# Splitting an RWKV stage into three pieces and emitting a block's channel mix behind the next block's time mix

## The chip, the cores and the metric

The kernel runs on one core of a Trainium2 chip. Its time is the device time of one execution in microseconds, the median of the runs shown. In this text PE is the matrix engine, DVE the vector engine, ACT the scalar engine, POOL the general engine (GpSimd), and SP the engine that only issues DMAs here.

## What is computed

An activation `x` of 64 sequences x 32 steps x 256 channels goes through six layers, each added to `x` (float32):

```python
x = x + L0_xattn(layernorm(x), ctx, ...)   # stage 0: cross attention over 257 context rows
x = x + L0_attn(layernorm(x), ...)         # stage 1: RWKV, the layer that the change is in
x = x + L0_ffn(layernorm(x), ...)          # stage 2: top-2 experts
x = x + L1_xattn(layernorm(x), ctx, ...)   # stage 3: quantized grouped attention
x = x + L1_attn(layernorm(x), ...)         # stage 4: Mamba
x = x + L1_ffn(layernorm(x), ...)          # stage 5: top-1 experts
```

RWKV has two halves. The time mix blends each step with the step before it, projects to k, v and r, runs a recurrence along the 32 steps in each channel, and multiplies by sigmoid(r); an output projection Wo is added to the normalized input. The channel mix normalizes that sum, blends with the step before again, and adds sigmoid(Wcr xr) * (Wcv relu(Wck xk)^2), where Wck goes from 256 to 1024 channels and Wcv back.

## The kernel before

The 2048 tokens are cut into four blocks of 512 tokens (16 sequences), as `x[b]`, 128 partitions x 4 x 256, which stay on the chip for the whole program. Each stage is a function that returns a `block(b)`; `layers` (from L1188) calls them in a written order. The blocks don't depend on each other, the stages of one block do.

What sets the order on the engines: each engine works its own queue in order. At build, a planner fills the queues from the instructions as they are emitted. Among those whose inputs and buffers are ready by its own cost figures, the one emitted first goes first. So the written order is a rank, not the order itself: in the trace matmuls of stage 0 and stage 1 stand in PE's queue in turns. A tile of a pool with `bufs=n` and a tag shares n buffers with the other tiles of that tag, and an instruction that takes a buffer waits for its last user. A stage's pools are opened on the left or the right side of the memory, and what is opened later on a side waits until the space is released.

Stage 0 (L136 to L321): a block loads four pieces of context (cn, cT; two buffers each), computes scores, a softmax and a weighted sum, and adds to x at L283. It also writes a quantized context and its step sizes to DRAM, which stage 3 reads. Its pools stand on the right side, so the weights of stages 2 and 3 can be loaded when its last block is done.

Stage 1 (L340 to L531), for a block: moments of x (DVE) and a reciprocal root (POOL and DVE); `norm_to` (L418) normalizes into rows `hn` (L429, DVE), transposes on PE (L123) and evacuates to `hT` (L422, ACT), a buffer that holds channels x 16 sequences x 33 steps with a zero ahead; `shift_mix` (L391) makes the difference `d` (L398) and the blends (L408) on DVE; `recur` (L432), once for each half of the channels, projects on PE (L415), evacuates on ACT (L435, L437, L439), and runs the recurrence on DVE with three scans (L443, L457, L458), a reciprocal (L464) and elementwise steps up to `rw` (L468), with products on POOL (L449, L461, L467); the output projection Wo (L490, PE), added on DVE (L491); a second norm and blend; the gate `sg` (L503 PE, L504 ACT). Then the channel mix: eight times a matmul pair L511 on PE, a relu L513 on ACT, a square L514 on POOL, and four matmuls L523 on PE into two banks; at the end the gate's product L528 on DVE and the sum L529 on POOL. Its pools stand on the left side, where stage 4 follows: stage 4's weights can be loaded when stage 1's last block has released the space.

Stage 2 (L537) adds its experts to x at L616. Stage 3 (L653) ends a block at L748. Stage 4 (L918) has a long recurrence that begins at L1036, stage 5 (L1081) writes the output.

The order in `layers`: stage 0 of block 0, then stage 0 of block b followed by stage 1 of block b - 1 while b is 1 or 2, stage 0 of block 3, the step sizes, stage 2 and stage 3 of block 0, stage 1 of blocks 2 and 3, and then stage 4's pools, stage 2 of block 1 and the rest.

Of the kernel before, what the change touches and what calls it, by code (L numbers as in the profile page):

```python
# [8 lines left out]
F32 = mybir.dt.float32  # L9
# [6 lines left out]
P = 128  # L16
NB, T, S, D = 64, 32, 257, 256
NTOK = NB * T
NT = NTOK // P
NBLK = 4  # L20
# [319 lines left out]
def _stage1(k, pool):  # L340
# [2 lines left out]


    nc, i = k.nc, k.i
    w, u, wk, sm1 = pool("w1", 1), pool("u1", 9), pool("wk1", 1), pool("small1", 2)
    pa, pb = pool("psa1", 2, space=bass.MemoryType.PSUM), pool("psb1", 2, space=bass.MemoryType.PSUM)
    wT = {n: _load_w(k, w, f"L0_attn_W{n}T", 2, D) for n in ("k", "v", "r", "o", "cr")}
    wck = _load_w(k, w, "L0_attn_WckT", 2, 4 * D)
# [11 lines left out]
    def padded(name, fill, shape=(16, T + 1)):  # L361
        t = w.tile([P, *shape], F32, name=name, tag=name)
        nc.gpsimd.memset(t, fill)
        return t

    wt, kp, e1b, e2b, e2bv = [], [], [], [], []
    for c in range(2):
        wt.append(padded(f"wt{c}", BIG))
        nc.vector.tensor_copy(wt[c][:, :, 1:], wdec[:, c : c + 1].unsqueeze(2).to_broadcast([P, 16, T]))
        kp.append(padded(f"kp{c}", BIG))  # L370
        e1b.append(padded(f"e1b{c}", 0.0))
        e2b.append(padded(f"e2b{c}", 0.0))
        e2bv.append(padded(f"e2bv{c}", 0.0))
    hT = padded("hT", 0.0, (2, 16, T + 1))

    def seq(t):
        return t.rearrange("p b t -> p (b t)")
# [8 lines left out]
        return pa.tile([P, BT], F32, name=name, tag="a")  # L386

    def rows(name):
        return wk.tile([P, 4, D], F32, name=name, tag="rows", bufs=3)

    def shift_mix(names):  # L391


        def mix(name):
            return wk.tile([P, 2, 16, T], F32, name=name, tag="mix", bufs=3)

        d = mix("d")
        nc.vector.tensor_tensor(  # L398
            d.rearrange("p c b t -> p (c b) t"),
            hT[:, :, :, 1:].rearrange("p c b t -> p (c b) t"),  # L400
            hT[:, :, :, 0:T].rearrange("p c b t -> p (c b) t"),
            ALU.subtract,
        )
        outs = []
        for n in names:
            o = d if n == names[-1] else mix("mix")
            for c in range(2):
                nc.vector.scalar_tensor_tensor(o[:, c], d[:, c], _chan(k, n, c), hT[:, c, :, 0:T], ALU.mult, ALU.add)  # L408
            outs.append(o.rearrange("p c b t -> p c (b t)"))
        return outs  # L410
# [4 lines left out]
            nc.tensor.matmul(p, wT[wname][:, c, o * P : (o + 1) * P], xT[:, c, :], start=c == 0, stop=c == 1)  # L415
        return p.rearrange("p (b t) -> p b t", t=T)

    def norm_to(xs, mean, scale, g, b):  # L418


        def evac(c, p):
            nc.scalar.activation(  # L422
                hT[:, c, :, 1:], p.rearrange("p (b t) -> p b t", t=T), AF.Identity,
                bias=_chan(k, b, c), scale=_chan(k, g, c),
            )

        hn = rows("hn")
        for j in range(4):
            nc.vector.tensor_scalar(hn[:, j, :], xs[:, j, :], mean[:, j, :], scale[:, j : j + 1], ALU.subtract, ALU.mult)  # L429
        _to_channels(k, [hn[:, j, :] for j in range(4)], evac, lambda shape, name: ps(name))  # L430
# [36 lines left out]
        nc.gpsimd.tensor_tensor(sr, sr, den, ALU.mult)  # L467
        nc.vector.tensor_tensor(rw[:, c].rearrange("p (b t) -> p b t", t=T), num, sr, ALU.mult)  # L468

    def block(b):  # L470
        x = k.x[b]
        xs = [x[:, j, :] for j in range(4)]


        mv = _moments(k, xs, "1", sm1)
        r8 = sm1.tile([P, 8], F32, name="r8", tag="r8")
        _rsqrt(k, r8, [(mv[:, :, 1], 1.0, LN_EPS), (mv[:, :, 1], 1.0 + LN_EPS, LN_EPS * LN_EPS)], "1", sm1)
        norm_to(x, mv[:, :, 0:1], r8[:, 4:8], "L0_attn_ln1_g", "L0_attn_ln1_b")
        xk, xv, xr = shift_mix(["L0_attn_tm_k", "L0_attn_tm_v", "L0_attn_tm_r"])
        rw = wk.tile([P, 2, BT], F32, name="rw", tag="rw", bufs=1)  # L480
        for c in range(2):
            recur(c, xk, xv, xr, rw)
        xn = rows("xn")
        for j in range(4):
            nc.gpsimd.tensor_scalar(xn[:, j, :], xs[j], mv[:, j, 0:1], r8[:, j : j + 1], ALU.subtract, ALU.mult)
        for j in range(0, 4, 2):
            p = pb.tile([P, 2, D], F32, name="wo", tag="b")
            for f in range(2):
                for c in range(2):
                    nc.tensor.matmul(p[:, f, :], rw[:, c, (j + f) * P : (j + f + 1) * P], wT["o"][:, c, :], start=c == 0, stop=c == 1)  # L490
            nc.vector.tensor_tensor(xn[:, j : j + 2, :], p, xn[:, j : j + 2, :], ALU.add)  # L491

        nc.gpsimd.tensor_tensor(x, x, xn, ALU.add)

        mv2, rstd2 = _stats(k, [xn[:, j, :] for j in range(4)], "1b", sm1)
        norm_to(xn, mv2[:, :, 0:1], rstd2, "L0_attn_ln2_g", "L0_attn_ln2_b")
        xk, xr = shift_mix(["L0_attn_cm_k", "L0_attn_cm_r"])
        sg = rows("sg")
        for j in range(0, 4, 2):
            p = pa.tile([P, 2, D], F32, name="cr", tag="a")  # L500
            for f in range(2):
                for c in range(2):
                    nc.tensor.matmul(p[:, f, :], xr[:, c, (j + f) * P : (j + f + 1) * P], wT["cr"][:, c, :], start=c == 0, stop=c == 1)  # L503
            nc.scalar.activation(sg[:, j : j + 2, :], p, AF.Sigmoid)  # L504

        cvs = [pb.tile([P, 2, D], F32, name="cv", tag="b") for _ in range(2)]

        def up(h):
            p = ps("ck")
            for c in range(2):  # L510
                nc.tensor.matmul(p, wck[:, c, h * P : (h + 1) * P], xk[:, c, :], start=c == 0, stop=c == 1)  # L511
            kk = wk.tile([P, BT], F32, name="kk", tag="kk", bufs=3)
            nc.scalar.activation(kk, p, AF.Relu)  # L513
            nc.gpsimd.tensor_tensor(kk, kk, kk, ALU.mult)  # L514
            return kk

        ahead = [up(0), up(1)]
        for h in range(8):
            if h + 2 < 8:
                ahead.append(up(h + 2))  # L520
            kk = ahead.pop(0)
            for j in range(4):
                nc.tensor.matmul(  # L523
                    cvs[j // 2][:, j % 2, :], kk[:, j * P : (j + 1) * P], wcv[:, h, :],
                    start=h == 0 and j % 2 == 0, stop=h == 7, skip_group_check=True,
                )
        for j in range(0, 4, 2):
            nc.vector.tensor_tensor(sg[:, j : j + 2, :], cvs[j // 2], sg[:, j : j + 2, :], ALU.mult)  # L528
        nc.gpsimd.tensor_tensor(x, x, sg, ALU.add)  # L529

    return block  # L531

# [653 lines left out]
def layers(k, out):  # L1188

    def opened(es, side):
        def pool(name, bufs, **kw):
            return es.enter_context(k.tc.tile_pool(name=name, bufs=bufs, side=side, reuse_waits="tile", **kw))

        return pool

    psum = dict(space=bass.MemoryType.PSUM)
    left0, left, right, right2 = ExitStack(), ExitStack(), ExitStack(), ExitStack()  # L1200
    with left0:
        s1 = _stage1(k, opened(left0, "left"))
        with ExitStack() as es:
            s0, steps = _stage0(k, opened(es, "right"))
            s0(0)
            for b in range(1, NBLK):
                s0(b)
                if b < NBLK - 1:
                    s1(b - 1)
            steps()  # L1210
        pool = opened(right, "right")
        k.small, k.ps, w3 = pool("small1", 2), pool("ps", 2, **psum), pool("w3", 1)
        k.wk3 = pool("wk3", 2)
        with ExitStack() as es:
            s3 = _stage3(k, w3, opened(es, "right")("tmp3", 1))
        s2 = _stage2(k, opened(right2, "right"))
        s2(0)
        s3(0)
        s1(NBLK - 2)
        s1(NBLK - 1)  # L1220
    with right, left:
        pool = opened(left, "left")
        k.psh, k.psp, k.psu = pool("psh", 2, **psum), pool("psp", 1, **psum), pool("psu", 1, **psum)
        w4 = pool("w4", 1)
        ahead, gates, recur = _stage4(k, w4, pool("wk4", 2))
        with right2:
            s2(1)
            v = {0: ahead(0)}
            gates(v[0])
            s3(1)  # L1230
            s2(2)
            v[1] = ahead(1)
            recur(0, v[0])
            s3(2)
            s2(3)
        k.psacc, w5 = pool("psacc", 2, **psum), pool("w5", 1)
        s5 = _stage5(k, w5, out)
        k.wk5 = pool("wk5", 2)
        for b in range(1, NBLK):
            gates(v[b])  # L1240
            if b + 1 < NBLK:
                v[b + 1] = ahead(b + 1)
            recur(b, v[b])
            if b + 2 < NBLK:
                s3(b + 2)
            s5(b - 1)
        s5(NBLK - 1)
# [81 lines left out]
```

## Time and profile before

| what | us |
|---|---|
| median of 3 runs | 2092.72 |
| lowest and highest run | 2090.38, 2098.58 |
| the profiled execution's own time | 2096.84 |
| its span, first to last instruction | 2095.1 |
| busy in the span: PE, DVE, POOL, ACT | 1644.2, 1391.0, 1013.9, 952.6 |

The profile is of one execution of the program. Its views used here: busy time of each engine in a stretch of the span (the columns are the stretch, its length, then for each engine busy us and number of instructions, the granted share of PE's clock, the DMA share and GB/s); waits (who waited for whom, total us, times, the longest); groups of instructions by source line (out<-in, shapes, count, then busy us and mean ns, then idle time of the engine ahead of them and who ended it); one line's instructions (min/median/max ns, and the start of the first and last in us); and the chain of work that ended last. PEld is PE's weight load, which overlaps with matmuls. Ends of matmuls are modelled. L490 is line 490 of the kernel.

### The profile page before, as it was taken

What the parts mean: (1) busy time and instruction counts of PE and PEld (TensorE: products, weight loads), DVE (VectorE), ACT (ScalarE), POOL (GpSimd) and SP (SyncE); (2) the same over time, 40 slices, a digit from 0 to 9 for tenths busy, and PEclk for the clock granted to TensorE, in tenths of its full rate; (3) what the DMA queues carried; (4) which work ended last, traced back from release to release, by engine and by line L of the source; (5) the groups of instructions that cost most, each with busy time, mean ns of one, the idle gap of its engine ahead of it and who ended that gap; (6) DMA issues with size and microseconds to landing.
All of it is one profiled execution on the core that took longest, in us unless ns stands there. A gap on an engine that the chain in (4) does not pass through costs nothing. (4 is left out here: it accounts for less than half of the span.)

```text
span 2095.1 us, 20245 instructions
## 1 busy us (share of the span) xinstructions
PE 1644.2 (78%) x6455; PEld 834.1 (40%) x6455; DVE 1391.0 (66%) x2444; ACT 952.6 (45%) x2009; POOL 1013.9 (48%) x1037
## 2 busy tenths in 40 slices
PE   4778966669979788656487798887888987787798
PEld 2334534335545434433234344433444433233343
DVE  5587584775584559889767988655888755876100
ACT  3445342304434174444146566356557445664232
POOL 4445445312121325667625777513767634998000
PEclk8677977889989898558687899888799887999799
DMA  7654232210001011121011232112232112332021
GB/s 239 219 182 144 91 120 80 79 34 21 21 21 43 17 42 51 30 61 61 0 50 53 80 91 90 31 41 65 71 88 73 49 31 66 89 111 77 30 81 40
DMA packets 87540, 149.93 MB, mean 72 GB/s; under 512 B 7672, under 2 KB 51978, under 8 KB 85386
## 3 DMA queue, kind: packets, MB, share of 16 engines
q1 hardware_dynamic: 84868, 147.69, 23.0%
q10 hardware_dynamic: 2566, 0.96, 0.2%
q8 instruction: 51, 0.84, 0.2%
q14 instruction: 55, 0.45, 0.1%
HBM read 137.71 MB, written 10.91 MB: 71 GB/s over the span
## 5 line engine op out<-in xcount | busy, mean ns | idle before, releaser
L1048 POOL TENSOR_TENSOR g<-dtx,bc 128x1024 f32<-128x1024 f32 x128 | 300.4, 2353 | 194.8 <-DVE h L1053 89.4
L1053 DVE TENSOR_TENSOR_SCAN h<-h,g 128x512 f32<-128x512 f32 x256 | 307.3, 1218 | 49.9 <-ACT h L1052 35.1
L1160 PE MATMUL up<-xT,w 128*128 128x512 f32 x512 | 288.1, 678 | 42.5 <-ACT hid L1162 37.3
L1055 POOL TENSOR_TENSOR xc<-xc,hc 128x1024 f32<-128x1024 f32 x128 | 301.0, 2356 | 26.5 <-DVE hc L1054 14.8
L1168 PE MATMUL acc<-hid,w 128*128 128x512 f32 x512 | 250.9, 610 | 15.8 <-ACT hid L1164 15.7
L1052 ACT ACTIVATE h<-dt,A 128x512 f32<-128x512 f32 x256 | 174.0, 692 | 184.5 <-DVE hc L1054 183.3
L1054 DVE TENSOR_TENSOR hc<-h,bc 128x512 f32<-128x512 f32 x256 | 169.7, 679 | 2.9 <-POOL xc L1055 0.5
L1160 PEld LDWEIGHTS up<-xT,w 128*128 128x128 f32 x512 | 97.3, 209 | 165.3 <-issue 79.2
L839 ACT ACTIVATE p<-sc,nm 128x256 f32<-128x256 f32 x256 | 117.6, 471 | 94.5 <-DVE nm L835 83.2
L1162 ACT ACTIVATE hid<-up,chan 128x512 f32<-128x512 f32 x128 | 87.2, 681 | 159.5 <-PE up L1160 159.4
L614 PE MATMUL weps<-we,xT 128*128 128x512 f32 x256 | 139.3, 665 | 17.2 <-DVE x L616 13.9
L1168 PEld LDWEIGHTS acc<-hid,w 128*128 128x128 f32 x512 | 94.1, 194 | 128.2 <-issue 96.3
L828 PE MATMUL sc<-kT,qm 32*128 32x256 f32 x512 | 131.6, 448 | 14.9 <-DVE od L867 11.5
L852 PE MATMUL pt_ps<-ident,p 128*128 128x128 f32 x512 | 97.0, 328 | 53.7 <-ACT p L839 26.6
L833 DVE TENSOR_REDUCE nm<-sc 128x2 f32<-128x512 f32 x128 | 86.3, 686 | 56.2 <-PE sc L828 55.1
L89 POOL TENSOR_TENSOR rs_t<-rs_r 128x4 f32<-128x4 f32 (+3 forms) x138 | 29.7, 218 | 183.1 <-DVE rs_r L87 157.0
L852 PEld LDWEIGHTS pt_ps<-ident,p 128*128 128x128 f32 x512 | 69.5, 165 | 107.1 <-ACT p L839 64.4
L828 PEld LDWEIGHTS sc<-kT,qm 32*128 32x128 f32 x512 | 81.5, 208 | 70.5 <-DVE od L867 20.7
L230 POOL TENSOR_TENSOR cT<-cT,scb 128x2056 f32<-128x2056 f32 x16 | 74.5, 4657 | 53.5 <-DMA scb<-scales 51.8
L1181 DVE SCALAR_TENSOR_TENSOR o<-rT,gt,x 128x256 f32<-128x256 f32 x16 | 7.7, 483 | 139.4 <-PE rT L1180 132.5
L854 ACT COPY pt<-pt_ps 128x512 f32<-128x512 f32 x128 | 74.0, 588 | 40.5 <-PE pt_ps L852 40.3
L514 POOL TENSOR_TENSOR kk<-kk 128x512 f32<-128x512 f32 x32 | 33.1, 1040 | 103.8 <-ACT kk L513 103.8
(389 smaller groups left out, 3218.7 us busy)
## 6 DMA issues: line engine op xcount, KB each, us to landing
bc<-rows SPq DMA_DIRECT2D x64, 512.0 KB
w<-in_L_ffn_w_dram SPq DMA_DIRECT2D x64, 512.0 KB
cT<-in_ctxT_dram SPq DMA_DIRECT2D x16, 1028.0 KB
cq<-cq SPq DMA_DIRECT2D x32, 514.0 KB
cn<-in_ctx_dram SPq DMA_DIRECT2D x64, 256.0 KB
scb<-scales SPq DMA_DIRECT2D x16, 514.0 KB
kb<-steps SPq DMA_DIRECT2D x16, 514.0 KB
x<-in_x_dram SPq DMA_DIRECT2D x4, 512.0 KB
```

Source lines behind the costliest of these rows:

```text
L614: nc.tensor.matmul(ps, xT[:, c, r], we[:, c, e : e + 2, :], start=c == 0, stop=c == 1)
L828: nc.tensor.matmul(sc[h][:, f, :], qm[r, e + f].rearrange("p l n g -> p (l n g)"), kTs[e][r, f, :], start=True, stop=True,)
L839: nc.scalar.activation(w_[:, f, h - h0, :], sc[h][:, f, :], AF.Exp, bias=nm[:, e + f, h : h + 1], accum_out=sm[:, e + f, h : h + 1],)
L852: nc.tensor.transpose(pt_ps[:, h, m, :], ws[e0, hp][:, f, h, m * P : (m + 1) * P], k.ident)
L1048: nc.gpsimd.tensor_tensor(g, dtx[:, c2 : c2 + 2], bc[:, 0:1, :].to_broadcast([P, 2, BT]), ALU.mult)
L1052: nc.scalar.activation(h, dt, AF.Exp, scale=A[:, c2 + c, n : n + 1])
L1053: nc.vector.tensor_tensor_scan(h, h, g[:, c, :], 0.0, ALU.mult, ALU.add)
L1054: nc.vector.tensor_tensor(hc[:, c, :], h, bc[:, 1, :], ALU.mult)
L1055: nc.gpsimd.tensor_tensor(y[:, c2 : c2 + 2], y[:, c2 : c2 + 2], hc, ALU.add)
L1160: nc.tensor.matmul(u, w1[e][:, c, q * P : (q + 1) * P], xT[:, c, :], start=c == 0, stop=c == 1)
L1162: nc.scalar.activation(hid[e][:, q, :], u, AF.Identity, bias=b1)
L1168: nc.tensor.matmul(acc[o], w2[e][:, q, o * P : (o + 1) * P], hid[e][:, q, :], start=n == H, stop=n == E * H + H - 1)
```

## The change

Stage 1's block function becomes three: `time_mix` (moments, norm, blend and recurrence), `between` (Wo, second norm, second blend, gate) and `channel_mix`. In `layers` the channel mix of block b - 1 is emitted behind the time mix of block b and ahead of the middle piece of block b. Stage 1 of a block is now emitted right behind stage 0 of the same block, ahead of stage 0 of the next one; stage 1 of block 2 up to its middle piece goes ahead of stage 0 of block 3; the time mix of block 3 and the channel mix of block 2 go between stages 2 and 3 of block 0; and stage 2 of block 1 goes ahead of the last channel mix and of stage 4's pools.

Buffers: `hT` gets a second copy, one for each norm. The rows (three buffers) and the blends (three buffers) share one tag with six. The recurrence's tiles have eight buffers, not nine. `e2bv` is one buffer for both halves of the channels, not two.

```diff
-    w, u, wk, sm1 = pool("w1", 1), pool("u1", 9), pool("wk1", 1), pool("small1", 2)
+    w, u, wk, sm1 = pool("w1", 1), pool("u1", 8), pool("wk1", 1), pool("small1", 2)
...
-        e2bv.append(padded(f"e2bv{c}", 0.0))
-    hT = padded("hT", 0.0, (2, 16, T + 1))
+        e2bv.append(e2bv[0] if c else padded("e2bv", 0.0))
+
+    hTs = [padded(f"hT{n}", 0.0, (2, 16, T + 1)) for n in range(2)]
...
     def rows(name):
-        return wk.tile([P, 4, D], F32, name=name, tag="rows", bufs=3)
-
-    def shift_mix(names):
+        return wk.tile([P, 4, D], F32, name=name, tag="rows", bufs=6)
+
+    def shift_mix(hT, names):
...
-            return wk.tile([P, 2, 16, T], F32, name=name, tag="mix", bufs=3)
+            return wk.tile([P, 2, 16, T], F32, name=name, tag="rows", bufs=6)
...
-    def block(b):
+    def time_mix(b):
...
-        norm_to(x, mv[:, :, 0:1], r8[:, 4:8], "L0_attn_ln1_g", "L0_attn_ln1_b")
-        xk, xv, xr = shift_mix(["L0_attn_tm_k", "L0_attn_tm_v", "L0_attn_tm_r"])
+        norm_to(hTs[0], x, mv[:, :, 0:1], r8[:, 4:8], "L0_attn_ln1_g", "L0_attn_ln1_b")
+        xk, xv, xr = shift_mix(hTs[0], ["L0_attn_tm_k", "L0_attn_tm_v", "L0_attn_tm_r"])
         rw = wk.tile([P, 2, BT], F32, name="rw", tag="rw", bufs=1)
         for c in range(2):
             recur(c, xk, xv, xr, rw)
+        return mv, r8, rw
+
+    def between(b, mv, r8, rw):
...
+        norm_to(hTs[1], xn, mv2[:, :, 0:1], rstd2, "L0_attn_ln2_g", "L0_attn_ln2_b")
+        xk, xr = shift_mix(hTs[1], ["L0_attn_cm_k", "L0_attn_cm_r"])
...
+        return xk, sg
+
+    def channel_mix(b, xk, sg):
+        x = k.x[b]
...
-        s1 = _stage1(k, opened(left0, "left"))
+        time_mix, between, channel_mix = _stage1(k, opened(left0, "left"))
         with ExitStack() as es:
             s0, steps = _stage0(k, opened(es, "right"))
-            s0(0)
-            for b in range(1, NBLK):
+
+            for b in range(NBLK - 1):
                 s0(b)
-                if b < NBLK - 1:
-                    s1(b - 1)
+                t = time_mix(b)
+                if b:
+                    channel_mix(b - 1, *c)
+                c = between(b, *t)
+            s0(NBLK - 1)
             steps()
...
         s2(0)
+        t = time_mix(NBLK - 1)
+        channel_mix(NBLK - 2, *c)
         s3(0)
-        s1(NBLK - 2)
-        s1(NBLK - 1)
+        c = between(NBLK - 1, *t)
+        s2(1)
+        channel_mix(NBLK - 1, *c)
...
         with right2:
-            s2(1)
             v = {0: ahead(0)}
```

## The prediction

> **What bounds the kernel now.** The page comes first. No engine is full (PE 78%, DVE 66%, POOL 48%), and the chain that ended last says nothing here: its shares add to 23% of the span and it starts only at 1611 us, in the Mamba and expert stages, far behind the edited code. So I read where each stage ends, from the start times by line. Stage 0's four blocks end (residual add L283) at 88, 175, 264 and 394 us. Stage 1 runs from 98 to 702. The first quantized-attention block ends (L748) at 714, and the first Mamba recurrence starts (L1036) at 768. From there it is 1327 us to the end, in which no instruction belongs to the change. So the question is when the part ahead of 714 is over. The busy times by stretch:
>
> ```profile
> core 0: us, PE busy (x) PEld busy (x) DVE busy (x) ACT busy (x) POOL busy (x), PEclk, DMA share, GB/s
> 0.00:400.00 400.00, 293.33 (x1263) 155.02 (x1264) 260.52 (x442) 162.23 (x476) 189.26 (x263) 0.79 0.45 147
> 400.00:714.00 314.00, 254.07 (x1234) 146.33 (x1233) 200.44 (x453) 107.54 (x279) 72.55 (x125) 0.89 0.10 31
> ```
>
> PE is busy 547 of 714 us and DVE 461: neither is the bound, so the two must be waiting for each other. Short stretches show where:
>
> ```profile
> 210.00:236.00 26.00, 25.76 (x91) 16.95 (x90) 3.02 (x9) 6.11 (x15) 11.16 (x11) 1.00 0.16 48
> 350.00:376.00 26.00, 24.75 (x87) 17.30 (x87) 3.23 (x4) 2.98 (x5) 9.60 (x12) 0.92 0.00 0
> 408.00:438.00 30.00, 4.03 (x13) 2.49 (x13) 28.55 (x43) 4.05 (x7) 6.48 (x12) 0.52 0.22 71
> ```
>
> The first two are channel mixes of RWKV blocks 0 and 1: PE full, DVE almost idle. The third is the recurrence of block 2: DVE full, PE idle. The waits of PE and of DVE name both sides (three answers: DVE in 88 to 240, DVE in 240 to 400, PE in 400 to 480; total, times, longest):
>
> ```profile
> DVE sg L528 <- PE cv L523: 22.9, 1, 22.9
> ...
> DVE sg L528 <- PE cv L523: 20.2, 2, 20.0
> ...
> PE wo L490 <- DVE rw L468: 26.0, 2, 13.5
> ```
>
> DVE stands 43 us before the channel mixes' products, PE stands 26 us before the output projection until the recurrence is done. From 480 to 714 PE is busy 206 of 234 us: what is left of RWKV, the experts and the attention block share it there.
>
> **The change part by part.** No arithmetic is added: each block has the same instructions. What moves is their rank in the queues, and I cost that in the part ahead of 714. Groups from 88 to 714 us (count, then busy, mean ns):
>
> ```profile
> L523 PE MATMUL cv<-w_L_attn_WcvT,kk 128*128 128x256 f32 x256 | 65.8, 394 | 8.8 <-POOL kk L514 8.8
> ...
> L511 PE MATMUL ck<-mix,w_L_attn_WckT 128*128 128x512 f32 x128 | 61.6, 601 | 0.0
> ...
> L490 PE MATMUL wo<-w_L_attn_WoT,rw 128*128 128x256 f32 x64 | 23.5, 508 | 41.9 <-DVE rw L468 41.9
> ```
>
> *(1) Channel mix of block b behind the time mix of b+1.* A channel mix holds PE for (65.8 + 61.6) / 4 = 32 us. Put beside the recurrence, it fits the hole of 26.0 us at 408 to 438: minus 26 behind stage 0, since PE is what limits 480 to 714. Today block 3's time mix can't slip in: its first norm is done at 488, but its transposes run at 543 and its mixing at 549, when block 2's channel mix has ended. The other PE stalls at L490 (41.9 in all, so 16 more) lie ahead of 394 and are counted in (3), not here.
>
> *(2) Block 2's time mix and middle piece now rank ahead of stage 0's block 3.* PE of these two pieces per block: projections (20.4 + 19.0 + 17.5) / 4 = 14.2, output projection 23.5 / 4 = 5.9, gate 17.9 / 4 = 4.5, transposes 13.3 / 4 = 3.3: 28 us. About 8 of it already runs before 394 today. So 20 us leave the stretch behind stage 0: minus 20.
>
> *(3) The price: stage 0 ends later.* Everything that opens on stage 0's memory (experts' and attention's weights) waits for its block 3. Its blocks took 87 us (175 - 88) ranked ahead of RWKV, 89 ranked behind block 0's RWKV, 130 behind block 1's. After the change all three rank behind a time mix and a middle piece. The DVE work that is pulled ahead is about 53 us a block (mixing and differences 12.6, norms 5.3, scans 8.2, reciprocals 6.7, the other recurrence steps 15.6, sums and statistics 5), of which 9 run before 394 already: 44, against the 43 us in which DVE stood before L528. Lower bound: all of it falls into that idle time, 0. Upper: three blocks at the worst rate seen, 88 + 3 x 130 = 478, plus 84. I take 95, 105 and 130, nearer to the rates seen than to three times the worst: end at 418, plus 24.
>
> *(4) Port of POOL and DVE.* Squarings L514 now run beside a recurrence. The trace has both sides (min/median/max ns):
>
> ```profile
> L466 DVE TENSOR_TENSOR aa<-aa,v x8: 658/678/5003, 138.8 to 605.2; 128x512 f32<-128x512 f32 x8
> ...
> L514 POOL TENSOR_TENSOR kk<-kk x32: 1032/1039/1085, 212.9 to 688.5; 128x512 f32<-128x512 f32 x32
> ```
>
> An add of 0.68 us took 5.0 when POOL's 4.5 us scaling of stage 0 ran: DVE stood for the whole of it. The Trainium skill ("SBUF — State Buffer", "Who interferes with whom") has this as a rule that speaks against the change: a DVE instruction with two SBUF inputs and a GpSimd one that reads SBUF exclude each other, and the later one blocks fully. By the rule, 24 squarings (three of four blocks have a time mix beside them) could each stop DVE for up to 1.04 us: plus 25. By the rows, squarings that had DVE work beside them still took 1.03 to 1.09, so POOL loses nothing, and DVE has a third of this part idle: the lower end is 0. I take 4.
>
> *(5) Second shifted buffer, six shared rows, eight in place of nine recurrence tiles, one e2bv.* Zero. A waiting channel mix holds two rows (xk, sg), the next time mix four (hn, d, two mixes): six. The shared e2bv makes chunk 1's product on POOL wait for chunk 0's last scan (L458), which stands earlier in DVE's queue than what that product needs anyway (POOL waited 33.5 us for ACT's e2b there). Without that cover: four scans of 1.36 us, 5 us. If rows run short, hn waits for a channel mix, as it does now; behind it on DVE would stand stage 0's softmax steps.
>
> *(6) Experts' block 1 ahead of the Mamba weights.* It already runs from 478 to 717, beside the attention block: zero. The last channel mix now ranks last, and Mamba's weight load on SP waits for it, as it did here (19.4 us for L511, issued at 687.8). RWKV pieces issue no DMAs; on SP the moved ones are stage 0's loads of block b+1, whose two buffers keep them ahead. Bounds -4 and +10; I take 0.
>
> Sum: -26 - 20 + 24 + 4 = -18. The profiled execution took 2096.84 (span 2095.1), 4.1 over the median of 2092.72. So 2096.8 - 18 = 2078.8, less 4.1: 2075.
>
> **Rivals.**
> *Stage 0 starves (slower).* One mechanism: DVE's and ACT's queues give RWKV's steps to the chip ahead of stage 0's softmax chain, and each block takes 110, 130, 130: end at 458, plus 64; 64 - 46 + 4 = +22: 2115. It decides from an end of stage 0 at 436 us (394 + 46 - 4). For it: the third block took 130 us with less ahead of it than it will have. Against: those 130 us hold 20 us of idle DVE.
> *The hole comes back (same).* Block 2's channel mix is spent as filler in stage 0, PE again waits at L490 with nothing else: the 26 us are lost and -20 + 24 + 4 = +8: 2101. PE's queue today alternates stage 0 and stage 1 matmuls from 110 to 127 us, so filling does happen early. Likewise if the written order hardly changes what each queue holds, as that alternation could suggest: 2093.
> *Full overlap (faster).* The 43 us of idle DVE take everything: stage 0 ends at 399, 5 - 46 + 4 = -37: 2056.
>
> **How the numbers follow.** Less than 0.5% (10 us) can't be told from no change here. The forecast has 0.40 (its own range 2062 to 2082), full overlap 0.15, the hole's return or no real change of order 0.17, starving 0.28 (2103 to 2138). Faster 0.55, same 0.17, slower 0.28; as cases of both signs matter, the range reaches into both: 2045 to 2118 leaves out a third of the full overlap and the worse half of the starving.
>
> **What would show it.** (1) PE's wait at L490 for L468 behind stage 0's end: under 8 us, not 26. DVE's waits L528 on L523: under 10 each, not 20 to 23. (2, 3) The last L283 at about 418; over 436 the rival holds. (4) L466 and L468 with more outliers of 1.5 to 2 us, none of them long. (6) L748's first block ending near 696, the first L1036 near 750, and 1327 us from there to the end, within 10. If that last distance moves by more, the reason lies in stages that I held fixed, and my sum is wrong even if the time is right.

## The result and the profile after

The changed kernel takes 2112.4 us (median of 6 runs, 2103.86 to 2114.12), the kernel before 2093.64 beside it (6 runs, 2090.38 to 2101.68): ratio 1.0077, 95% interval 1.0052 to 1.0103. It became slower. The forecast was 2075; the time lies inside the range, on the wrong side of no change.

The head of the page after, which answers to the busy times of before (PE 1644.2, DVE 1391.0, POOL 1013.9):

```profile
span 2110.0 us, 20265 instructions
...
PE 1664.8 (79%) x6455; PEld 849.5 (40%) x6455; DVE 1379.5 (65%) x2444; ACT 955.2 (45%) x2009; POOL 1036.4 (49%) x1037
```

The counts are the same. PE is busy 21 us longer with the same matmuls, POOL 23 us, DVE 11 us shorter. Where in the span does the loss come about? The stretches are cut at four milestones: the end of stage 0 (last L283), the end of the first attention block (L748 before, L759 after), the end of the last recurrence, and the end. Before, then after:

```profile
core 0: us, PE busy (x) PEld busy (x) DVE busy (x) ACT busy (x) POOL busy (x), PEclk, DMA share, GB/s
0.00:394.00 394.00, 289.46 (x1249) 153.01 (x1250) 254.97 (x427) 159.82 (x472) 184.64 (x245) 0.78 0.45 146
394.00:714.00 320.00, 257.95 (x1249) 148.34 (x1248) 206.00 (x468) 109.95 (x282) 77.16 (x142) 0.89 0.11 35
714.00:1915.00 1201.00, 942.40 (x3591) 462.42 (x3590) 909.14 (x1492) 633.76 (x1201) 733.89 (x601) 0.83 0.21 60
1915.00:2095.00 180.00, 154.38 (x371) 70.33 (x370) 20.90 (x60) 49.11 (x54) 18.17 (x50) 0.90 0.16 50
```

```profile
0.00:431.00 431.00, 314.95 (x1305) 167.81 (x1305) 283.62 (x476) 177.56 (x494) 217.26 (x270) 0.79 0.41 134
431.00:751.00 320.00, 281.24 (x1273) 159.55 (x1272) 194.43 (x489) 95.57 (x264) 70.61 (x141) 0.87 0.11 34
751.00:1922.00 1171.00, 907.59 (x3510) 448.10 (x3510) 880.79 (x1423) 632.91 (x1197) 730.56 (x578) 0.83 0.22 62
1922.00:2110.00 188.00, 161.03 (x370) 74.00 (x368) 20.70 (x60) 49.11 (x54) 17.94 (x49) 0.86 0.15 48
```

Read the second column, the length. Stage 0 ends 37 us later. The stretch behind it, where I had put my whole gain of 46 us, is 320 us in both (in two further executions of each it was 311 us after and 322 before, both times). Of the 37 us the middle gives back 30, where less work is left (PE 908 us instead of 942), and the last stretch, which the change does not touch, adds 8. PE did more in the 320 us, not less: 281 us instead of 258. The experts' matmuls alone, in this stretch before and after:

```profile
L614 PE MATMUL weps<-we,xT 128*128 128x512 f32 x125 | 64.1, 640 | 2.4 <-DVE rs_v L84 0.9 <-DVE x L616 0.9 <-DVE x L610 0.5
```

```profile
L625 PE MATMUL weps<-we,xT 128*128 128x512 f32 x168 | 89.6, 664 | 5.1 <-DVE x L627 3.0 <-DVE rs_r L86 2.0
```

The waits that I wanted to remove did vanish. PE's waits in 400 to 500 us, all of the answer above 1.5 us, and then DVE's in 240 to 400 us (total, times, longest):

```profile
PE gT_ps L613 <- DVE pr L610: 7.4, 1, 7.4
PE pt_ps L259 <- ACT s L251: 6.1, 1, 6.1
PE prj L416 <- DVE mix L409: 3.8, 1, 3.8
PE tps L123 <- DVE xn L115: 2.1, 1, 2.1
PE pt_ps L260 <- POOL pl L256: 1.9, 1, 1.9
PE av_ps L265 <- ACT pt L263: 1.9, 2, 1.3
```

```profile
DVE x L283 <- PE o_ps L281: 13.6, 3, 8.2
DVE sg L539 <- PE cv L534: 8.7, 4, 4.6
```

The output projection (now L497) waits nowhere behind stage 0, where it had waited 26.0 us. DVE's 20.2 us before the gate's product are 8.7 (in 88 to 240 us, where they were 22.9, the answer has no such line). In their place stage 0's own last step heads the list: L283 now waits 13.6 us for PE in this window, 3.4 before. So the change did what it says, and the time went the other way.

### The profile page after: what moved, and what is told of

Read it like the earlier page. It is cut to its first block, busy times and chain, and to the rows that moved or that the text cites. A ratio compares the mean times of both kernels' runs of the same rounds, so it can differ in the third digit from the quotient of the medians.

```text
span 2110.0 us, 20265 instructions
## 1 busy us (share of the span) xinstructions
PE 1664.8 (79%) x6455; PEld 849.5 (40%) x6455; DVE 1379.5 (65%) x2444; ACT 955.2 (45%) x2009; POOL 1036.4 (49%) x1037
## 5 line engine op out<-in xcount | busy, mean ns | idle before, releaser
L1171 PE MATMUL up<-xT,w 128*128 128x512 f32 x512 | 283.8, 668 | 37.2 <-ACT hid L1173 33.8
L1065 DVE TENSOR_TENSOR hc<-h,bc 128x512 f32<-128x512 f32 x256 | 169.8, 679 | 2.9 <-POOL xc L1066 0.7
L625 PE MATMUL weps<-we,xT 128*128 128x512 f32 x256 | 147.4, 697 | 22.3 <-DVE x L627 15.9
L839 PE MATMUL sc<-kT,qm 32*128 32x256 f32 x512 | 136.3, 463 | 10.5 <-DVE od L878 5.3
L525 POOL TENSOR_TENSOR kk<-kk 128x512 f32<-128x512 f32 x32 | 39.7, 1246 | 132.7 <-ACT kk L524 125.2
```

What stands on the lines that cost most here:

```text
L625: nc.tensor.matmul(ps, xT[:, c, r], we[:, c, e : e + 2, :], start=c == 0, stop=c == 1)
L839: nc.tensor.matmul(sc[h][:, f, :], qm[r, e + f].rearrange("p l n g -> p (l n g)"), kTs[e][r, f, :], start=True, stop=True,)
L1065: nc.vector.tensor_tensor(hc[:, c, :], h, bc[:, 1, :], ALU.mult)
L1171: nc.tensor.matmul(u, w1[e][:, c, q * P : (q + 1) * P], xT[:, c, :], start=c == 0, stop=c == 1)
```

## The experiments

All milestones are of the profiled execution, in us. "Distance" is from the end of stage 0 to the end of the first attention block; "PE share" is PE's busy share of the time up to the end of stage 0; "last rec." is the end of the last recurrence. The ratio is the measured one, with its interval, to the kernel before as it ran beside each group of kernels (2093.64 us beside the change, 2097.19 beside e1 to e4, 2094.40 beside e5 to e8, 2095.05 beside e9 to e12); it is not the quotient of two rows.

| kernel | stage 0 ends | PE share | first attention ends | distance | last rec. ends | median | ratio |
|---|---|---|---|---|---|---|---|
| before | 394 | 0.73 | 714 | 320 | 1915 | 2093.64 | 1 |
| after | 431 | 0.73 | 751 | 320 | 1922 | 2112.40 | 1.0077 [1.0052, 1.0103] |
| e1 stage 0 first | 363 | 0.74 | 735 | 372 | 1907 | 2105.97 | 1.0030 [1.0017, 1.0044] |
| e2 buffers only | 391 | 0.74 | 719 | 328 | 1917 | 2093.14 | 0.9983 [0.9969, 0.9996] |
| e3 thin channel mix | 361 | 0.69 | 685 | 324 | 1859 | 2038.79 | 0.9708 [0.9688, 0.9729] |
| e4 attention first | 433 | 0.73 | 744 | 311 | 1923 | 2113.77 | 1.0087 [1.0057, 1.0117] |
| e5 skew, old places | 361 | 0.73 | 683 | 322 | 1899 | 2082.87 | 0.9930 [0.9901, 0.9960] |
| e6 new ranks, no skew | 487 | 0.71 | 803 | 316 | 1977 | 2162.14 | 1.0311 [1.0280, 1.0342] |
| e7 experts' 1 put back | 430 | 0.73 | 735 | 305 | 1913 | 2102.47 | 1.0035 [1.0021, 1.0049] |
| e8 experts' 1 on before | 393 | 0.74 | 713 | 320 | 1909 | 2092.79 | 0.9991 [0.9969, 1.0014] |
| e9 e5 with one hT | 365 | 0.73 | 685 | 320 | 1901 | 2082.10 | 0.9943 [0.9916, 0.9969] |
| e10 stage 0 outright first | 309 | 0.73 | 669 | 360 | 1898 | 2078.88 | 0.9912 [0.9883, 0.9941] |
| e11 skew, one place later | 324 | 0.70 | 680 | 356 | 1897 | 2073.14 | 0.9889 [0.9855, 0.9923] |
| e12 e5 + experts' 1 moved | 365 | 0.73 | 689 | 324 | 1899 | 2083.28 | 0.9934 [0.9913, 0.9956] |

**Which part costs.** My theory after the result: the price is the rank that RWKV's pieces gained over stage 0. Rivals: the buffers, the skew itself, and PE's load.

*e1*, the changed kernel with stage 0's next block ranked ahead again:

```diff
+            s0(0)
             for b in range(NBLK - 1):
-                s0(b)
+                s0(b + 1)
+                if b == NBLK - 2:
+                    steps()
                 t = time_mix(b)
...
-            s0(NBLK - 1)
-            steps()
```

> The three pieces and all buffers as changed; only stage 0 of each block is emitted one step earlier, ahead of the time mix that trails it, as it was before the change (blocks 2's time mix, channel mix 1 and middle piece now rank just behind stage 0 of block 3). Theory (stage 0's rank is the price; from its end to the end of the first attention block it is a fixed chain of about 320 us): stage 0 ends near 394 to 405, the first attention block ends at 714 to 730, the time falls to 2085 to 2100. Rival (the buffers or the channel mix beside the recurrence slow everything): stage 0 still ends after 425 and the time stays near 2110.

Stage 0 ended at 363, even ahead of the 394 to 405 that the theory gave: rank sets that end. But there is no fixed chain of 320 us behind it: the attention block followed 372 us later, with block 2's pieces now ranked between the two, and ended at 735, past the theory's 730. The time missed the theory's 2085 to 2100 as well: 0.30% of the 0.77% of loss stayed (the profiled execution, 2096.84, was 9 us under this kernel's median). Rank matters at both places.

*e2*, the new buffers with the old order (the shared rows, second hT, eight tiles, one e2bv):

> The changed buffers (second hT, six shared rows, eight recurrence tiles, one e2bv) with the three pieces called one behind the other in the order of before. Theory (buffers cost nothing): 2093 within 6, stage 0 ends at 394 within 6, the first attention block ends at 714 within 8. Rival (shared rows or the one e2bv cause waits): 2100 to 2112, with longer waits of DVE or POOL ahead of 714.

0.9983 [0.9969, 0.9996]: the buffers cost nothing in the old order, so the loss lies in the new one.

*e3*, the kernel before with a quarter of the channel mix (six of its eight hidden slices are left out):

```diff
-        for h in range(8):
-            if h + 2 < 8:
+        for h in range(2):
+            if h + 2 < 2:
...
-                    start=h == 0 and j % 2 == 0, stop=h == 7, skip_group_check=True,
+                    start=h == 0 and j % 2 == 0, stop=h == 1, skip_group_check=True,
```

> The kernel before, with the channel mix cut to 2 of its 8 hidden slices (the other 6 are left out: about 24 us of PE work in each block, 72 of it behind 394 us less some 22 for block 0 and 1 ahead of it). The forecast's reading (PE's work limits 480 to 714): the first attention block ends 40 us or more earlier, near 670, and the time falls by 40 or more, to 2050. Theory (a chain through experts' block 0 and attention block 0 sets it): it ends at 700 to 710 and the time falls by less than 20.

This run decides what my step (1) rested on. Of the four channel mixes two lie behind stage 0, so about 2 x 32 x 6/8 = 48 us of PE's work left that stretch (in the traces their two groups of matmuls, L511 and L523, fall from 66.5 to 16.3 us there). Its window, and the experts' matmuls up to 685 us:

```profile
361.00:689.00 328.00, 261.32 (x1214) 144.33 (x1212) 233.52 (x570) 106.38 (x274) 72.22 (x159) 0.87 0.11 34
...
L614 PE MATMUL weps<-we,xT 128*128 128x512 f32 x192 | 97.7, 633 | 7.7 <-DVE x L616 2.8 <-DVE rs_r L86 1.5 <-DVE mv L102 1.3
```

328 us up to 689, 4 us past the last L748 of the block: 324 us, no shorter than before. PE is busy 261 us in it all the same: work of lower rank filled it, the experts' 97.7 us instead of 64.1 above all. So the PE time of RWKV is not what limits this stretch; what does, this run doesn't show. The total nevertheless fell by 58 us, as the forecast's reading had it and not by under 20 as my theory had it, but by another way: stage 0 ended 33 us earlier, and later stages found work already done.

*e4*, the changed kernel with the attention block ranked ahead of block 3's time mix and block 2's channel mix:

```diff
         s2(0)
+        s3(0)
         t = time_mix(NBLK - 1)
         channel_mix(NBLK - 2, *c)
-        s3(0)
```

> The changed kernel, with the time mix of block 3 and the channel mix of block 2 emitted behind the first attention block in place of ahead of it. Theory (the recurrence of block 3 sits in DVE's queue between the experts' small steps and stretches that chain): from stage 0's end (431) to the first attention block's end it takes 290 to 305 us in place of 320, and the time falls to 2095 to 2105. Rival (chain is set by PE's work in this part): 320 us again, and 2110.

The distance is 311 us, as in two of the three executions of the changed kernel, not the 290 to 305 that I expected, and the time is the changed kernel's (1.0087). That these two pieces rank ahead of the attention block is not the price.

**Skew and rank apart.** The change makes two moves at once: the channel mix goes behind the next time mix (the skew), and all pieces move up (the ranks). e5 has the skew alone, e6 the ranks alone. e5, against the changed kernel:

```diff
-            for b in range(NBLK - 1):
+            s0(0)
+            for b in range(1, NBLK):
                 s0(b)
-                t = time_mix(b)
-                if b:
-                    channel_mix(b - 1, *c)
-                c = between(b, *t)
-            s0(NBLK - 1)
+                if b < NBLK - 1:
+                    t = time_mix(b - 1)
+                    if b > 1:
+                        channel_mix(b - 2, *c)
+                    c = between(b - 1, *t)
             steps()
...
         s2(0)
-        t = time_mix(NBLK - 1)
-        channel_mix(NBLK - 2, *c)
         s3(0)
-        c = between(NBLK - 1, *t)
-        s2(1)
+        for b in range(NBLK - 2, NBLK):
+            t = time_mix(b)
+            channel_mix(b - 1, *c)
+            c = between(b, *t)
         channel_mix(NBLK - 1, *c)
```

e6, against the changed kernel:

```diff
+            def s1(b):
+                channel_mix(b, *between(b, *time_mix(b)))
             for b in range(NBLK - 1):
                 s0(b)
-                t = time_mix(b)
-                if b:
-                    channel_mix(b - 1, *c)
-                c = between(b, *t)
+                s1(b)
...
-        t = time_mix(NBLK - 1)
-        channel_mix(NBLK - 2, *c)
         s3(0)
-        c = between(NBLK - 1, *t)
-        s2(1)
-        channel_mix(NBLK - 1, *c)
+        s1(NBLK - 1)
```

In both, the experts' block 1 is back behind the gathers (`s2(1)` ahead of `ahead(0)`).

> The skew alone: the channel mix of block b is ranked behind the time mix of block b+1, with the buffers of the changed kernel, but each RWKV piece keeps the place that its block had before (block 3's stage 0 ahead of the pieces of block 2, the experts' first block ahead of them, the experts' block 1 behind the gathers). Theory A (the price is the rank that the RWKV pieces gain over stage 0 and over the first attention block): stage 0 ends at 390 to 400, the first attention block's last feed-forward eviction at 705 to 720, the time 2080 to 2094. Rival B (the price is the skew itself: two channel mixes in flight hold VectorE and GpSimd): stage 0 still ends at 390 to 400, but the time is 2104 to 2114 as in the changed kernel.

> The rank alone: RWKV blocks 0 to 2 whole, no skew, all ranked ahead of stage 0's last block, block 3 ahead of the first attention block; buffers of the changed kernel, experts' block 1 behind the gathers as before. Theory A (rank is the price): stage 0 ends at 425 to 445, the first attention block at 740 to 755, the time 2104 to 2114. Rival B (the skew is the price): stage 0 ends late as well, but the time is 2088 to 2097, as before.

(In e6 as run, block 3 ranks behind the first attention block, not ahead of it as its expectation says.) e7 is the changed kernel with only the experts' block 1 put back, e8 the kernel before with only that block moved ahead. e7's edit, which e8 makes the other way round:

```diff
-        s2(1)
         channel_mix(NBLK - 1, *c)
...
         with right2:
+            s2(1)
             v = {0: ahead(0)}
```

> The changed kernel with one thing put back: the experts' block 1 is ranked behind the gathers and loads of the Mamba stage again. If this place is what lengthens the tail (400 us instead of 392 from the last attention block to the end), the time is 2098 to 2104. If it costs nothing, as I predicted, 2108 to 2114 and a tail of 400.

> The kernel before with that one edit alone: the experts' block 1 ranked ahead of the gathers and loads of the Mamba stage. If the place costs nothing, 2088 to 2098 and a tail of 392 us; if it is what lengthens the tail, 2100 to 2105 and a tail near 400.

With e2 (old ranks, no skew) these make a square, all with the new buffers and the experts' block 1 in its old place (the kernel before had 2097.19 beside e2 and 2094.40 beside the others; e7 alone has block 3's time mix ahead of the attention block):

| median us | no skew | skew |
|---|---|---|
| old ranks | 2093.14 (e2) | 2082.87 (e5) |
| new ranks | 2162.14 (e6) | 2102.47 (e7) |

The skew gains in either row (10 and 60 us); the ranks lose in either column (69 and 20). The rival that the skew is the price falls. Theory A holds in direction only: e6 loses 69 us where I had expected 11 to 21. Stage 0's end tells how; e5, e6 and e7, up to it and on to the attention block:

```profile
0.00:361.00 361.00, 263.14 (x1170) 132.23 (x1170) 246.11 (x424) 161.14 (x474) 183.11 (x232) 0.81 0.50 161
361.00:683.00 322.00, 285.03 (x1311) 166.07 (x1312) 205.71 (x465) 109.08 (x282) 88.64 (x155) 0.89 0.11 32
```

```profile
0.00:487.00 487.00, 344.40 (x1403) 189.47 (x1403) 292.91 (x486) 182.03 (x501) 214.75 (x278) 0.77 0.37 120
487.00:803.00 316.00, 265.12 (x1203) 143.88 (x1202) 192.22 (x498) 89.85 (x255) 62.23 (x133) 0.85 0.10 33
```

```profile
0.00:430.00 430.00, 313.29 (x1305) 166.27 (x1305) 285.57 (x477) 177.87 (x495) 217.03 (x270) 0.80 0.42 134
430.00:735.00 305.00, 267.62 (x1272) 153.27 (x1272) 194.87 (x483) 95.21 (x263) 69.99 (x141) 0.91 0.11 36
```

Divide PE's busy time in a first row by its length: 263/361, 344/487, 313/430 are 0.73, 0.71, 0.73. Stages 0 and 1 mixed keep PE at 0.69 to 0.74 in all fourteen kernels, whatever their order. (DVE's share varies more, from 0.60 to 0.71.) So I read it thus: stage 0 ends once the RWKV work ranked ahead of its last block is done too, at about that rate, and each us of PE work pulled ahead costs about 1/0.73 = 1.4 us. That is an average. From e11 (below; 227 us of PE work ahead of an end at 324) by way of e5, the kernel before and the changed one to e6, the end moves by 163 us for 117 us of PE work, 1.4 each, but step by step by 1.0, 1.3, 1.5 and 1.9; and from e10 (309) to e11 it moves 15 us for only 3 of PE. The skew lowers that amount by one channel mix, which slips behind stage 0. e5's end at 361 instead of my expected 390 to 400 comes from this: stage 0 has PE's 263 us ahead of its end, the kernel before 289. That the share is so steady is an observation; why it is 0.73 and not more was not taken apart.

On e8 the moved experts' block costs nothing; in the changed kernel it makes up the difference between 1.0077 and 1.0035, some 10 us. It is not the tail that I had suspected (from the last attention block's end, 1697, to 2098 us it is still 401 us in e7): the first attention block ends at 735, against 751, 743 and 745 in three executions of the changed kernel.

**Does the rule carry further.** If stage 0's end is what counts, stage 0 should rank higher still. e9 is e5 with one buffer of shifted activations:

```diff
-    hTs = [padded(f"hT{n}", 0.0, (2, 16, T + 1)) for n in range(2)]
+    hTs = [padded("hT", 0.0, (2, 16, T + 1))] * 2
```

e10 puts stage 0 outright first; its order up to block 2's pieces, which follow as in e5:

```diff
+            for b in range(NBLK):
+                s0(b)
+            steps()
+            c = between(0, *time_mix(0))
...
+        t = time_mix(1)
+        channel_mix(0, *c)
         s2(0)
         s3(0)
+        c = between(1, *t)
```

e11 puts RWKV one place later than e5:

```diff
+            for b in range(NBLK - 1):
+                s0(b)
+            c = between(0, *time_mix(0))
+            s0(NBLK - 1)
             steps()
+            t = time_mix(1)
+            channel_mix(0, *c)
+            c = between(1, *t)
...
         s2(0)
         s3(0)
```

e12 is e5 with the experts' block 1 moved as in the change:

```diff
             c = between(b, *t)
+        s2(1)
         channel_mix(NBLK - 1, *c)
...
-            s2(1)
             v = {0: ahead(0)}
```

> The skew in the old places (the run that was faster) with one buffer of shifted activations instead of two: the channel mix's input of block b and the time mix's input of block b+1 share it. If the second buffer is needed for the skew, 2090 or more and stage 0 or the first attention block later by 5 us and more; if it only spares a wait that other work covers, 2080 to 2088.

> The skew, with all four blocks of stage 0 ranked ahead of every RWKV piece, and the experts' and attention's first block ranked behind the channel mix of block 0, ahead of all other pieces. Theory A (the end of stage 0 sets the first attention block, which follows it by 305 to 322 us): stage 0 ends at 310 to 350, the first attention block at 630 to 672, the time 2045 to 2075. Rival B (what is not done beside stage 0 has to be done later, on engines that are then short): stage 0 ends early too, but the first attention block follows it by 340 us or more, or later stages give it back, and the time is 2083 or more.

> The skew with the RWKV pieces one place lower than in the faster run: block 0's time mix behind stage 0's block 2, block 1's behind block 3. Theory A: stage 0 ends at 335 to 355, the first attention block at 645 to 675, the time 2055 to 2080. Rival B: 2083 or more, with the first attention block over 322 us behind stage 0.

> The skew in the old places, with the experts' block 1 ranked ahead of the last channel mix, as in the changed kernel. On the kernel before this place cost nothing, in the changed kernel 10 us. If it is the skew that makes it cost (block 3's channel mix then lies behind the experts' block 1), the first attention block comes 10 to 15 us later and the time is 2090 to 2096; if it costs only where stage 0 ends late, 2080 to 2086.

e9: the second buffer is not needed, 2082.10 against 2082.87. e12: 2083.28, so the moved experts' block costs only in the changed kernel, not with the skew as such. e10 and e11 end stage 0 at 309 and 324, earlier than I expected, but then the distance grows past 340 us, as the rival had it; their times lie with theory A (e11) and between the two (e10, whose 2079 is over theory A's 2075 and under the rival's 2083). The stretch behind stage 0 in e11 and in e10:

```profile
324.00:680.00 356.00, 302.51 (x1405) 181.98 (x1404) 225.19 (x508) 124.06 (x302) 116.55 (x189) 0.91 0.08 26
```

```profile
309.00:669.00 360.00, 299.94 (x1360) 179.11 (x1360) 231.45 (x510) 120.40 (x300) 112.18 (x188) 0.89 0.09 30
```

So 305 to 328 us is no constant. With e10's stage 0 at 309, block 0's channel mix ends only at 343, and the experts' first block needs it. Still both are faster than the kernel before: **of the kernels that leave nothing out e11 has the lowest median, 2073.14 us, ratio 0.9889 [0.9855, 0.9923]**, 1.1% under the kernel before. Its interval overlaps those of e10 and of e5, so that the lower rank gains on e5's is likely and not shown.

**The last 8 us.** In the last stretch the changed kernel's PE was busy 161 us instead of 154 with the same matmuls. In short stretches, before and after, the last output projection (L1065, L1076 after) looks like this:

```profile
1914.00:1918.00 4.00, 3.06 (x6) 1.21 (x5) 4.00 (x3) 0.69 (x1) 4.00 (x3) 0.57 0.00 0
1918.00:1928.00 10.00, 9.72 (x35) 6.08 (x36) 4.52 (x14) 0.00 (x0) 2.32 (x4) 1.00 0.00 0
```

```profile
1922.00:1926.00 4.00, 1.41 (x5) 0.82 (x4) 3.16 (x3) 0.69 (x1) 4.00 (x4) 0.95 0.00 0
1926.00:1940.00 14.00, 14.00 (x30) 8.01 (x28) 3.10 (x9) 0.00 (x0) 1.11 (x2) 0.53 0.01 1
```

The granted clock falls to half for one short piece before (0.57 over 4 us is 3.4 us at half), for 13.7 us after (0.53 over 14 us is 13.2, 0.95 over the 4 us ahead another 0.4). The projection, from its first to its last matmul, takes 19.8 us instead of 13.3. e1, e4 and e7, which differ from the changed kernel in one place each, have the same 184.9 us from the end of the last recurrence to the last output, all other kernels 174.6 to 179.3. Further executions of the two kernels, with nothing changed, were to tell whether it is the kernel's or the execution's:

> The changed kernel once more, as it is. If the half clock at the end belongs to the kernel, 184 to 186 us from the end of the last recurrence to the last output, the last output projection 19 to 20 us, span 2105 to 2113. If it belonged to the one execution, 174 to 180 us and 13 to 18.

> The kernel before once more, as it is. If the stretch is the kernel's own, 174 to 178 us from the end of the last recurrence to the last output; if it varies from run to run, it may be up to 185.

> The changed kernel a third time, with the same expectation as for its second look: 184 to 186 us if the stretch is the kernel's own, 174 to 180 if it is the execution's.

> The kernel before a third time, with the same expectation as for its second look: 174 to 178 us if the stretch is the kernel's own, up to 185 if it is the execution's.

Changed kernel: 184.9 and 179.6 (times 2108.4, 2105.76). Before: 176.6 and 174.6 (2095.17, 2094.55). So it is mostly the kernel's, by 3 to 10 us, and differs by some us from one execution to the next. Over all 18 traces it goes with the length of the half-clocked piece: 3.4 us and a stretch of 174.6 to 176.7, 6.8 and 177.8 (e11), 10.2 and 179.2 to 179.6 (e5, e9, the third execution of the changed kernel), 13.7 and 184.9 (the other five). The last recurrence ends at 1918.5 and 1921.2 us in the changed kernel and at 1913.5 and 1915.0 in the kernel before. As means over three executions of each, the changed kernel is 6 us late there (1920.6 against 1914.5), what is left of the late stage 0, and takes 7 us more behind it (183.1 against 176.0): 13 of the 16 us that the ratio gives. What makes the clock fall just there for this order stays open; nothing was run that changes the clock alone.

## Why the prediction was wrong, step by step

- *What bounds.* That neither engine is full and the two wait for each other was right. That the part ahead of 714 can be costed by adding up PE's free and busy time was not.
- *(1), minus 26, and (2), minus 20: the failed step is "since PE is what limits 480 to 714".* The hole was filled and the waits went, as named. Summed over its instructions, RWKV's PE time in the stretch fell from 145 to 119 us. But the experts' rose from 98 to 141 us, and of the 46 us the stretch gave 0 in the first execution and 11 in the two others; in e3 it kept 324 us with about 48 us of PE work taken out. The freed time went to work that nobody waited for yet: the experts' block 2 (L627) adds its results between 714 and 800 us, between 763 and 830 before. High busy time had been read as a limit; it was filling. What does set the 305 to 328 us of most orders stays open.
- *(3), plus 24: right in kind, too small.* Measured plus 37. I let the 44 us of DVE work that moves ahead run inside DVE's idle 43 us. DVE's waits did vanish, but PE had 25.5 us more work ahead of stage 0's end (289.5 to 315.0), and at its share of 0.73 that alone makes 35 us. The rates that I took (95, 105, 130) were 102, 120 and 120.
- *(4), plus 4: direction right, one side not priced.* I took POOL to lose nothing and DVE to pay. Both paid; the squarings after (33.1 us and 1040 ns before), and one step of the recurrence, before (L462) and after (L463):

```profile
L525 POOL TENSOR_TENSOR kk<-kk 128x512 f32<-128x512 f32 x32 | 39.7, 1246 | 132.7 <-ACT kk L524 125.2 <-ACT rt L903 7.4
...
L462 DVE TENSOR_TENSOR bb<-e,bb x8: 657/678/1601, 136.1 to 599.3; 128x512 f32<-128x512 f32 x8
...
L463 DVE TENSOR_TENSOR bb<-e,bb x8: 658/1596/1611, 127.1 to 483.6; 128x512 f32<-128x512 f32 x8
```

  Of the 32 squarings 14 took 1.38 to 2.09 us, each beside a step of DVE that reads two tiles from SBUF, and such steps took up to 1.6 us instead of 0.68. The rows that I had read could not show it: in the kernel before not one of the 32 squarings has a step of the recurrence beside it. The Trainium skill's rule ("SBUF — State Buffer", "Who interferes with whom") says that the one that comes second waits, either way round; the trace fits it, and I had applied it to one side only. The price is small. The squarings cost POOL 6.6 us more, but PE's waits for them are 5.0 us, 8.8 before; and stage 1's steps on DVE take 6 us less in all, since four of them, not seven, stood for over 4 us beside POOL's scaling of stage 0.
- *(5), zero: right* (e2). In e5's order the second hT is not needed (e9).
- *(6), zero: right on the kernel before (e8), wrong in the changed one*, by some 10 us (e7): my reading, which e12 fits and no run isolates, is that with stage 0 late the experts' block 1, ranked ahead of the last channel mix, competes with an attention block that is already late.
- *The distance of 1327 us to the end, "within 10": failed.* The first recurrence started 32 us later (800) and the rest took 1310, 17 less; the experts were ahead by then. By my own rule the sum is wrong even where the time agrees. The rival that starves stage 0 had the right direction, RWKV's rank delays stage 0, and at 2115 nearly the right time; but the time is luck, since it came by other terms. It had an end at 458 and kept the 46 us of gain; in truth the end was 431 (432 and 433 in two more executions), short of the 436 that was to decide for it, the gain was 0 to 11, and some 30 us came back later.

## What to carry to other kernels

Emission rank is a budget: work pulled ahead of a stage delays that stage at about the rate at which the engines really run together (here on average 1.4 us for each us of PE), even if it seems to fit another engine's idle time. Before a hole is booked as a gain, ask which work takes the freed time and whether anyone waits for that work; e3, which simply removes part of it, is a cheap test. And split an edit that moves two things: here the skew alone was 0.7% faster (with a lower rank 1.1%), while both moves together were 0.8% slower.

## What the runs showed of the hardware

The clock of PE fell to half in the last output projection, though PE was busy for 14.00 of 14 us there, after a wait for POOL of 2.6 us (L1076 for L1069); before, a wait of 2.1 us was followed by a half-clocked piece of only some 3.4 us. The changed kernel had such a wait too, 2.15 us up to 1919.6, and kept the full clock until 1925.6, so the length of the wait alone doesn't decide. The Trainium skill ("TensorE: Matmul & The Clock Gate", "Part 1: The HAM clock gate") has full clock return after one busy window of about 3.4 us; here, counting PE as busy as the profile does, it took 13.7 us, about four of them, and the same matmuls (128x256) took a mean of 575 ns instead of 414.
